# Wu products in 32-column tiles with two-block halo rows, against layers 1 and 2 on (row, channel) partitions

## The chip, the cores and the metric

The kernel runs on one core of one Trainium2 chip. The metric is the device time of one execution in microseconds (us); lower is better. The two kernels compute the same function; this document compares the kernel "before" with the kernel "after" that the diff below makes of it.

## The reference

The input x is 32 images of 8 channels and 256 x 256 pixels, float32. Four layers follow one another, each of the form x = x + f(groupnorm(x)) with four groups of two channels:

```python
# layer 0, on n = groupnorm(x)
grid = n
for _ in range(15):                       # the automaton, each channel by itself
    mapped = 3.9 * grid * (1 - grid)
    grid = 0.85 * (0.7 * mapped + 0.3 * conv3x3(mapped, K_local)) + 0.15 * n
cml = clip(grid)
nca = sigmoid(Wu @ relu(conv3x3(n, Wp) + bp) + bu)     # 8 -> 128 -> 8 channels
g = sigmoid(Wg2 @ relu(conv3x3([n, cml, nca], Wg1) + bg1) + bg2)
x = x + g * cml + (1 - g) * nca
x = x + conv3x3(quantize(groupnorm(x)), quantize(w1)) / scale + b1   # layer 1, scale over all of x
x = x + conv3x3(groupnorm(x), w2) + b2                              # layer 2
x = x + conv5x5(groupnorm(x), w3), every channel by itself          # layer 3
```

## The kernel before, in words

There are two stages. Layer 1 needs the largest absolute value over all images, so layer 0 of every image is finished first (stage 1, the first `with` block) and layers 1 to 3 follow (stage 2, the second block).

**Stage 1** has two streams of work, written as two generators. `lattice(b)` runs the automaton of image b. It loads the image into `xb` (L231), takes the statistics (L237 and `group_stats`, whose two small products are L94 and L101), writes the normalised image to DRAM (`xn_d`, `nr_d`), turns it to a layout of patches by transposes (L259) and does 15 steps. In a step each of the 8 channels gets two products, one with `patch_sb` (L281) and one with `ring_sb` (L282), and VectorE finishes the cell update (L289, L291). The rims of the patches travel by DMA from `state` to `rings` (`spread`, L221, on SyncE's queue). At the end the state is turned back (L302), copied into `xb` (L305) and written to DRAM (`cr_d`, L311).

`gated(b)` does the rest of layer 0. The image is cut into 16 blocks of 16 rows; `hidden(r2)` takes two blocks at a time. For each of the 16 row offsets it makes one product with Wp (L360: 72 rows of the moving tile `im`, out `ph` of 128 hidden channels x 512 pixels), ScalarE's Relu into `hh` (L365), and one product with Wu (L344). Wu has only 8 outputs, so before places them by a shifted window of a wide weight tile: all 16 offsets accumulate into one full 128-partition tile `pn`, each filling its 8 rows and adding zeros to the others. `gate(r2)` makes nine products with Wg1 (L393), two with the rows of the neighbouring blocks (L398 reads `ha`, L399 reads `hb`), one with Wg2 (L404), and the mixture on POOL and VectorE (L411 to L418). `beside_two` fills `hb` by DMA from `nh` (L321).

The two streams are woven: each `yield` of `lattice` carries a load, and the gated stream is advanced to 1.2 images behind. A scheduler then reorders the instructions of each engine by their expected times, so the order that runs isn't exactly the order written.

**Stage 2** keeps an image as (row, channel) on the partitions: partition 8 r + c holds channel c of row r of every block, the free axis holds the 16 blocks. A 3x3 convolution then takes three products with all 128 rows, one for each column shift (L499), and a fourth with a tile of 48 neighbouring rows that a DMA has gathered (`beside`, L128; product L503). So `conv3` is four products for each of eight chunks of 512 pixels, in bf16 for layer 1 and in float32 for layer 2. Layer 3 takes the image by whole rows (y, two halves of 128 rows): five products with `w3_sb` (L578) and a sixth with the few rows across the seam (`xr2`, L569 and L582). The output of layer 2 goes through DRAM (`x3_d`, L547) to get to that layout (`y`, L554). The loop runs layer 3 of image b-3, layer 2 of image b-1 and layer 1 of image b:

```python
for b in range(B + 3):
    if b >= 3:
        layer3(b - 3, *threes.pop(b - 3))
    if 1 <= b <= B:
        threes[b - 1] = layer2(b - 1, *twos.pop(b - 1))
    if b < B:
        twos[b] = layer1(b)
```

Of the kernel before, what the change touches and what calls it, by code (L numbers as in the profile page):

```python
# [9 lines left out]
F32 = mybir.dt.float32  # L10
BF16 = mybir.dt.bfloat16
# [49 lines left out]
def kernel(  # L61
    ctx, tc, x, patch, ring, wp, bp, wu, bu, wg1, wga, wgb, bg1, wg2, bg2, w1, b1, w2, b2, w3,
    w3h, eye, gavg, gavr, gsel, out,
# [12 lines left out]

    gavg_sb = const(keep, gavg, [P, P], "gavg_sb")
    gavr_sb = const(keep, gavr, [P, P], "gavr_sb")
# [8 lines left out]
    x3_d = [dram.tile([P, NPX], F32, name=f"x3_d{b}") for b in range(2)]  # L87
# [35 lines left out]
    def beside(queue, t, src, q):  # L123


        row, long = HB * WP, (HB - 1) * WP - 2
        for i, (p, to, at) in enumerate(((P - C, 1, 0), (0, 0, 1))):
            queue.dma_start(  # L128
                t[q + 24 * i : q + 24 * i + 24, :, :].rearrange("p k w -> p (k w)")[
                    :, to * WP : to * WP + long  # L130
                ],
                window(src, p * row + at * WP, [[row, C], [1, 3], [1, long]]),
            )
# [19 lines left out]
    with ExitStack() as es:  # L153
# [13 lines left out]
        wu_sb = const(wt, wu, [P, 2 * P - C], "wu_sb")  # L167
# [6 lines left out]
        bg2_sb = const(wt, bg2, [P, 1], "bg2_sb")  # L174

# [13 lines left out]
        nh = wt.tile([P, HB, WP], F32, name="nh")  # L189
        ha = wt.tile([96, HB, WP], F32, name="ha")  # L190
        hb = wt.tile([72, HB, WP], F32, name="hb")
        state = wt.tile([P, C, SN], F32, name="state")
        rings = [wt.tile([RING, 4, SN], F32, name=f"rings{i}") for i in range(2)]
        for t in (xb, nh, ha, hb, state, *rings):
            nc.gpsimd.memset(t, 0.0)
# [3 lines left out]
        xn_d = [dram.tile([C, HP, WP], F32, name=f"xn_d{i}") for i in range(3)]  # L199
        xr_d = [dram.tile([P, HB, W], F32, name=f"xr_d{i}") for i in range(3)]  # L200
        nr_d = [dram.tile([P, HB, WP], F32, name=f"nr_d{i}") for i in range(3)]
        cr_d = [dram.tile([P, HB, WP], F32, name=f"cr_d{i}") for i in range(3)]
# [24 lines left out]
        def lattice(b):  # L227
# [5 lines left out]
                on_rows(xr_d[b % 3], W), x[b].rearrange("c (k r) w -> (c k) r w", k=HB)  # L233
            )
            bn = small.tile([P, RB, 6], F32, name="bn0")
            for r in range(RB):
# [3 lines left out]
            yield 3  # L240
# [10 lines left out]
                window(xn_d[b % 3], WP, [[HP * WP, C], [RB * WP, HB], [1, RB * WP]]),  # L251
                xb.rearrange("p r w -> p (r w)"),
            )
            nc.gpsimd.dma_start(on_rows(nr_d[b % 3], WP), xb)
            yield 3
            for t4 in range(TX // 4):
                ps = psum.tile([P, 512], F32, name="ps")
                for j in range(4):
                    nc.tensor.transpose(  # L259
                        ps[:, bass.ts(j, P)], flat[:, bass.ts(4 * t4 + j, P)], eye_sb  # L260
                    )
                nc.scalar.copy(flat[:, bass.ts(t4, 512)], ps)
                if t4 % 4 == 3:
                    yield 0.5
# [9 lines left out]
            yield 1  # L274
            for step in range(STEPS):
                for half in range(2):
# [21 lines left out]
                    yield 1  # L298
            for t4 in range(TX // 4):
# [9 lines left out]
                if t4 % 4 == 3:  # L309
                    yield 0.5  # L310
            nc.gpsimd.dma_start(on_rows(cr_d[b % 3], WP), xb)  # L311

        LATTICE = 6 + 0.5 * TX // 16 + 1 + 2 * STEPS + 0.5 * TX // 16

        def beside_two(r2):

            row = HB * WP
            for i, (p, k0, to) in enumerate(((P - C, 2 * r2, 2 * r2 + 1), (0, 2 * r2, 2 * r2 - 1))):
                skip, last = max(0, -to), max(0, to + 2 - HB)
                long = (2 - skip - last) * WP - 2  # L320
                nc.sync.dma_start(  # L321
                    hb[24 * i : 24 * i + 24, :, :].rearrange("p k w -> p (k w)")[
                        :, (to + skip) * WP : (to + skip) * WP + long
                    ],
                    window(nh, p * row + (k0 + skip) * WP, [[row, C], [1, 3], [1, long]]),
                )

        def gated(b):
# [3 lines left out]
            xn, xr, nr, cr = xn_d[b % 3], xr_d[b % 3], nr_d[b % 3], cr_d[b % 3]  # L332
            beside(nc.gpsimd, ha, nr, 0)
            beside(nc.gpsimd, ha, cr, 48)
# [4 lines left out]
            def hidden(r2):  # L339
                pn = ps_n.tile([P, 512], F32, name="psn")  # L340
                late = None

                def second(hh, r):
                    nc.tensor.matmul(  # L344
                        pn, wu_sb[:, C * (RB - 1 - r) : C * (RB - 1 - r) + P], hh,
                        start=r == 0, stop=r == RB - 1,
                    )

                for half in range(2):
# [8 lines left out]
                    for j in range(8):  # L358
                        ph = psum.tile([P, 512], F32, name="ph", tag="ps")
                        nc.tensor.matmul(  # L360
                            ph.rearrange("p (k w) -> p k w", w=W), wp_sb,
                            im[:, :, j * WP : j * WP + W], start=True, stop=True,
                        )
                        hh = hp.tile([P, 512], F32, name="hh")
                        nc.scalar.activation(hh, ph, AF.Relu, bias=bp_sb)  # L365
                        if late is not None:
                            second(*late)
                        late = (hh, 8 * half + j)
                        yield
                second(*late)  # L370
                nc.scalar.activation(  # L371
                    nh[:, 2 * r2 : 2 * r2 + 2, 1 : 1 + W],
                    pn.rearrange("p (k w) -> p k w", w=W), AF.Sigmoid, bias=bu_sb,
                )
                beside_two(r2)
# [3 lines left out]
            def gate(r2):  # L379
                k0 = 2 * r2  # L380
                if r2 % 2 == 0:
# [9 lines left out]
                for s, src in enumerate((xq, cq, nh[:, k0 : k0 + 2, :])):  # L391
# [7 lines left out]
                nc.tensor.matmul(o, wgb_sb, hb[:, k0 : k0 + 2, 0:W], start=False, stop=True)  # L399
                g1 = hp.tile([P, 512], F32, name="g1", tag="hh")  # L400
# [4 lines left out]
                gt = hp.tile([P, 2, W], F32, name="gt", tag="hh")  # L405
                nc.scalar.activation(gt.rearrange("p r w -> p (r w)"), pq, AF.Sigmoid, bias=bg2_sb)  # L406
                ci = cq[:, :, 1 : 1 + W]
                ni = nh[:, k0 : k0 + 2, 1 : 1 + W]
# [18 lines left out]
            st = stat1[:, b, :]  # L427
# [6 lines left out]
            nc.vector.tensor_reduce(peak1[:, b : b + 1], ext2, AX.X, ALU.max, apply_absolute_value=True)  # L434
        GATED = NCH * (RB + 5)

        done = 0
        rest = (None for b in range(B) for _ in gated(b))  # L440
        for b in range(B):
            at = 0
            for load in lattice(b):
                at += load
                due = ((b - 1.2) * LATTICE + at) * GATED / LATTICE
                while done < due:
                    next(rest)
                    done += 1
        for _ in rest:
            pass  # L450


    with ExitStack() as es:
        wt = es.enter_context(tc.tile_pool(name="wt1", bufs=1))
        two = es.enter_context(tc.tile_pool(name="two", bufs=2))
        psum = es.enter_context(tc.tile_pool(name="ps_b", bufs=3, space=PSUM))
        ps_v = es.enter_context(tc.tile_pool(name="ps_v", bufs=5, space=PSUM))

        w1_sb = const(wt, w1, [P, 4, P], "w1_sb")
        b1_sb = const(wt, b1, [P, 1], "b1_sb")  # L460
        w2_sb = const(wt, w2, [P, 4, P], "w2_sb")
        b2_sb = const(wt, b2, [P, 1], "b2_sb")
        w3_sb = const(wt, w3, [P, 5, P], "w3_sb")
        w3h_sb = const(wt, w3h, [72, 2, P], "w3h_sb")
# [16 lines left out]
        w1_bf = wt.tile([P, 4, P], BF16, name="w1_bf")  # L481
        quantize(w1_bf.rearrange("p a b -> p (a b)"), w1f, sc[:, 1:2])


        qh = wt.tile([P, HB, WP], BF16, name="qh")
        qb = wt.tile([72, HB, WP], BF16, name="qb")
        xh = wt.tile([P, HB, WP], F32, name="xh")
        xb2 = wt.tile([72, HB, WP], F32, name="xb2")

        xr = wt.tile([P, 2, C, W + 4], F32, name="xr")  # L490
        xr2 = wt.tile([72, C, W + 4], F32, name="xr2")
        for t in (qh, qb, xh, xb2, xr, xr2):
            nc.gpsimd.memset(t, 0.0)

        def conv3(src, near, w, i):
            ps = ps_v.tile([P, 512], F32, name="psv")
            o = ps.rearrange("p (k w) -> p k w", w=W)
            for dx in range(3):
                nc.tensor.matmul(  # L499
                    o, w[:, dx, :], src[:, 2 * i : 2 * i + 2, dx : dx + W],  # L500
                    start=dx == 0, stop=False,
                )
            nc.tensor.matmul(  # L503
                o, w[0:72, 3, :], near[:, 2 * i : 2 * i + 2, 0:W], start=False, stop=True
            )
            return ps

        def layer1(b):
            x1 = two.tile([P, NPX], F32, name="x1")
            nc.gpsimd.dma_start(x1, x1_d[b])  # L510
            for k in range(4):
# [6 lines left out]
                    qh[:, 4 * k : 4 * k + 4, 1 : 1 + W],  # L518
                    t.rearrange("p (r w) -> p r w", w=W), sc[:, 0:1],
                )  # L520
            beside(nc.sync, qb, qh, 0)
            x2 = two.tile([P, NPX], F32, name="x2")
            bn = small.tile([P, NCH, 6], F32, name="bn")
            for i in range(NCH):
                ps = conv3(qh, qb, w1_bf, i)
                c = x2[:, bass.ts(i, 512)]
                nc.scalar.activation(c, ps, AF.Identity, bias=b1_sb, scale=sc[:, 3:4])
                nc.vector.tensor_tensor(c, c, x1[:, bass.ts(i, 512)], ALU.add)
                nc.vector.bn_stats(bn[:, i, :], c)
            st = small.tile([P, 2], F32, name="st2")  # L530
            group_stats(psum, bn, st, gavr_sb)
            return x2, st

        def layer2(b, x2, st):
            nc.vector.tensor_scalar(  # L535
                xh[:, :, 1 : 1 + W], x2.rearrange("p (k w) -> p k w", w=W),
                st[:, 0:1], st[:, 1:2], ALU.subtract, ALU.mult,
            )
            beside(nc.sync, xb2, xh, 0)
            bn = small.tile([P, NCH, 6], F32, name="bn")  # L540
            for i in range(NCH):
                ps = conv3(xh, xb2, w2_sb, i)
                c = x2[:, bass.ts(i, 512)]
                nc.vector.scalar_tensor_tensor(c, ps, b2_sb, c, ALU.add, ALU.add)
                nc.vector.bn_stats(bn[:, i, :], c)
            x3 = x3_d[b % 2]
            nc.gpsimd.dma_start(x3, x2)  # L547
# [185 lines left out]
```

## Time and profile before

| | us |
|---|---|
| median of three runs | 21494.88 |
| lowest and highest run | 21493.68 to 21496.85 |
| the profiled execution: its own time | 21493.68 |
| its span, first to last instruction | 21491.9 |
| stage 1, by the last product of layer 0 | 0 to 18940 |
| stage 2 | 18940 to 21492 |

The span is the profiler's; 1.8 us of the execution lie around it. PE is the engine of matrix products, PEld its weight load, DVE the vector engine, ACT the scalar engine, POOL and SP the two that mostly issue DMAs here. A float32 product shows as two MATMUL instructions, a bf16 product as one. "Busy" of PE counts from the start of a product to its modelled end and products overlap, so the time that a product costs is read from the distance between the starts of neighbours in the timeline, not from its mean duration.

### The profile page before, as it was taken

Reading aid. Unit: us, or ns where it says so; the run is one execution under the profiler, and the core shown is the slowest. Engines: PE = TensorE matmul, PEld = TensorE weight load, DVE = VectorE, ACT = ScalarE, POOL = GpSimd, SP = SyncE. Lnnn points to the kernel's source line nnn. Section 1 sums busy time; section 2 is a strip of 40 time slices with the busy share of each in tenths; the row PEclk is TensorE's granted clock in tenths of the full one; section 3 lists DMA queues with packets and bytes.
Section 4 is the critical chain, followed back from the end, with each engine's and each line's share of the span. In section 5 each row is a group of like instructions: output and inputs, shape, how many; then the busy total and the mean of one; then the engine's idle time right before and its main releaser. Section 6 shows DMA issues by size and latency. Waiting matters only on the chain.

```text
span 21491.9 us, 137690 instructions
## 1 busy us (share of the span) xinstructions
PE 19778.0 (92%) x46664; PEld 8662.7 (40%) x46664; DVE 8103.2 (38%) x13657; ACT 4075.8 (19%) x5790; POOL 1570.3 (7%) x1649
## 2 busy tenths in 40 slices
PE   6899999999999999999999999999999999989999
PEld 2343443434343444444343434344443434434444
DVE  4333333333333333333333333333333333245554
ACT  0111222212212111222222212121122222211110
POOL 0000000000000000000000000000000000011111
PEclk8999999999999999999999999999999999999999
DMA  5444444444444444444444444444444444345554
GB/s 112 104 104 105 103 109 106 107 108 108 105 109 106 108 103 106 105 105 108 105 110 107 107 106 108 107 106 102 105 106 108 107 107 105 84 106 126 126 126 109
DMA packets 525150, 2307.92 MB, mean 107 GB/s; under 512 B 111468, under 2 KB 179540, under 8 KB 356388
## 3 DMA queue, kind: packets, MB, share of 16 engines
q1 hardware_dynamic: 213668, 835.31, 21.3%
q10 hardware_dynamic: 172032, 810.61, 13.3%
q0 software_dynamic: 138752, 653.18, 11.5%
q8 instruction: 377, 6.18, 0.1%
q14 instruction: 321, 2.63, 0.0%
HBM read 1129.33 MB, written 471.38 MB: 74 GB/s over the span
## 4 chain that ended last, share of the span: by engine, by line
PE 79%; issue 8%; DMA 7%; DVE 3%; POOL 1%; ACT 1%; SPq 0%; ACTq 0%; POOLq 0%; DVEq 0%
PE ph L360 15%; PE psn L344 15%; PE psc L282 14%; PE psc L281 14%; PE pg L393 7%; PE psv L578 5%; PE psv L499 4%; DMA rings<-state 2%; DMA hb<-nh 2%; DMA xb<-in_x 1%; PE psv L503 1%; PE pq L404 1%; PE psv L582 1%; PE pg L399 1%; PE pg L398 1%
## 5 line engine op out<-in xcount | busy, mean ns | idle before, releaser
L289 DVE SCALAR_TENSOR_TENSOR state<-psc,dr 128x512 f32<-128x512 f32 x3840 | 2620.8, 689 | 7462.1 <-PE psc L282 5203.8
L365 ACT ACTIVATE hh<-ph,bp_sb 128x512 f32<-128x512 f32 x4096 | 2812.6, 687 | 8527.0 <-PE ph L360 7196.7
L360 PE MATMUL ph<-im,wp_sb 72*128 72x512 f32 x8192 | 4301.8, 622 | 26.6 <-DMA im<-xn_d 14.1
L282 PE MATMUL psc<-rings,ring_sb 80*128 80x512 f32 x7680 | 4006.9, 607 | 325.5 <-issue 271.6
L344 PE MATMUL psn<-hh,wu_sb 128*128 128x512 f32 x8192 | 4255.1, 612 | 21.8 <-ACT hh L365 21.7
L281 PE MATMUL psc<-state,patch_sb 128*128 128x512 f32 x7680 | 3932.0, 597 | 117.5 <-DVE state L289 115.5
L360 PEld LDWEIGHTS ph<-im,wp_sb 72*128 72x128 f32 x8192 | 1614.7, 199 | 2063.1 <-issue 1449.1
L344 PEld LDWEIGHTS psn<-hh,wu_sb 128*128 128x128 f32 x8192 | 1565.4, 194 | 2182.1 <-issue 1841.7
L291 DVE SCALAR_TENSOR_TENSOR state<-state 128x512 f32<-128x512 f32 x3584 | 2387.4, 695 | 30.5
L282 PEld LDWEIGHTS psc<-rings,ring_sb 80*128 80x128 f32 x7680 | 1478.6, 194 | 2215.4 <-issue 2194.8
L281 PEld LDWEIGHTS psc<-state,patch_sb 128*128 128x128 f32 x7680 | 1448.5, 190 | 2047.9 <-issue 1696.9
L413 DVE TENSOR_TENSOR gt<-gt,nh 128x512 f32<-128x512 f32 x256 | 177.9, 695 | 3176.7 <-POOL gt L412 3176.7
L412 POOL TENSOR_TENSOR gt<-gt,df 128x512 f32<-128x512 f32 x256 | 328.9, 1285 | 12404.6 <-ACT gt L406 11178.1
L578 PE MATMUL psv<-xr,w_sb 128*128 128x512 f32 x2560 | 1159.9, 595 | 0.5 <-DVE xr L563 0.5
L401 ACT ACTIVATE g<-pg,bg_sb 128x512 f32<-128x512 f32 x256 | 176.3, 689 | 3642.6 <-PE pg L399 3185.5
L94 PE MATMUL ps<-mv,gavg_sb 128*128 128x1 f32 x64 | 17.8, 348 | 785.1 <-DVE mv L92 785.1
L393 PE MATMUL pg<-xq,wg_sb 128*128 128x512 f32 x1536 | 713.4, 596 | 0.0
L499 PE MATMUL psv<-xh,w_sb 128*128 128x512 f32 x1536 | 704.1, 595 | 8.1 <-DVE xh L535 4.1
L578 PEld LDWEIGHTS psv<-xr,w_sb 128*128 128x128 f32 x2560 | 475.5, 189 | 565.5 <-issue 561.1
L393 PE MATMUL pg<-nh,wg_sb 128*128 128x512 f32 x1536 | 701.2, 592 | 0.0
L393 PE MATMUL pg<-cq,wg_sb 128*128 128x512 f32 x1536 | 701.0, 592 | 0.0
L411 POOL TENSOR_TENSOR df<-cq,nh 128x512 f32<-128x512 f32 x256 | 436.6, 1706 | 2127.7 <-ACT nh L371 2021.2
(132 smaller groups left out, 9430.8 us busy)
## 6 DMA issues: line engine op xcount, KB each, us to landing
im<-xn_d ACTq DMA_DIRECT2D x3072, 193.3 KB
rings<-state SPq DMA_DIRECT2D x1920, 213.8 KB
rings<-state SPq DMA_DIRECT2D x1920, 142.5 KB
xn_d<-xb POOLq DMA_DIRECT2D x32, 2064.0 KB, 23.6
nr_d<-xb POOLq DMA_DIRECT2D x32, 2064.0 KB, 29.4
xq<-nr_d ACTq DMA_DIRECT2D x128, 516.0 KB
cr_d<-xb POOLq DMA_DIRECT2D x32, 2064.0 KB, 11.2
cq<-cr_d ACTq DMA_DIRECT2D x128, 516.0 KB
```

The lines of the kernel that those rows point to most:

```text
L281: nc.tensor.matmul(o, patch_sb[:, c, :], v, start=True, stop=False)
L282: nc.tensor.matmul(o, ring_sb[:, c, :], rings[half][:, c % 4, 0 : TX * SY].rearrange("p (x y) -> p x y", y=SY)[:, :, 0:TY], start=False, s ...
L289: nc.vector.scalar_tensor_tensor(v, o, FLOOR, dr[:, c], ALU.max, ALU.add)
L291: nc.vector.scalar_tensor_tensor(v, v, 1.0, v, ALU.subtract, ALU.mult)
L344: nc.tensor.matmul(pn, wu_sb[:, C * (RB - 1 - r) : C * (RB - 1 - r) + P], hh, start=r == 0, stop=r == RB - 1,)
L360: nc.tensor.matmul(ph.rearrange("p (k w) -> p k w", w=W), wp_sb, im[:, :, j * WP : j * WP + W], start=True, stop=True,)
L365: nc.scalar.activation(hh, ph, AF.Relu, bias=bp_sb)
L393: nc.tensor.matmul(o, wg1_sb[:, s, dx, :], src[:, :, dx : dx + W], start=s == dx == 0, stop=False,)
L411: nc.gpsimd.tensor_tensor(df, ci, ni, ALU.subtract)
L412: nc.gpsimd.tensor_tensor(gt, gt, df, ALU.mult)
L499: nc.tensor.matmul(o, w[:, dx, :], src[:, 2 * i : 2 * i + 2, dx : dx + W], start=dx == 0, stop=False,)
L578: nc.tensor.matmul(o, w3_sb[:, dx, :], xr[:, k, 2 * g : 2 * g + 2, dx : dx + W], start=dx == 0, stop=False,)
```

## The change

The diff has five parts.

1. **Wu in column tiles** (`hidden`, `second`). The weight tile becomes four windows of 32 columns. The products of four row offsets go out together, two to partitions 32 q of `pn` and two to partitions 32 (q + 1), alternating between the two tiles. `hh` gets six buffers, and `g1`/`gt` a tag of their own with three.
2. **Halo rows for two blocks** (`beside_two`, `hbs`). `nh` gets an empty block at each end, and `hb` becomes two small tiles, each for the two blocks of one `gate`, filled at the start of `gate`.
3. **The weave** of stage 1: `gated(b - 1)` runs wholly inside `lattice(b)`, every `yield` weighing the same; the DRAM tiles go from three to two.
4. **Layers 1 and 2 by (channel, block)** on the partitions: partition 16 c + k. A 3x3 convolution is nine products, one for each tap, over 18 rows of which the first and last are fetched by `halo` (two products with a shift matrix and a ScalarE copy). The statistics of layer 0 are carried to that layout by a product with `tob`.
5. **Layer 3** takes ten products for each chunk (five with its own half, five with the other), in place of six; the loop runs layer 3 of image b-2; the loads and stores of stage 2 go to SyncE's queue, and `y` comes in two DMAs in place of sixteen.

```diff
-                def second(hh, r):
-                    nc.tensor.matmul(
-                        pn, wu_sb[:, C * (RB - 1 - r) : C * (RB - 1 - r) + P], hh,
-                        start=r == 0, stop=r == RB - 1,
-                    )
+                def second():
+                    for hh, r in late:
+                        q, i = divmod(r, 4)
+                        nc.tensor.matmul(
+                            pn[32 * q : 32 * q + 32, :], wu_sb[:, i, :], hh,
+                            start=i == 0, stop=i == 3,
+                        )
+                    late.clear()
...
-                    for j in range(8):
+                    for rows in ((0, 4, 1, 5), (2, 6, 3, 7)):
+                        four = []
+                        for i, j in enumerate(rows):
...
+                            hh = hp.tile([P, 512], F32, name="hh", bufs=6)
+                            nc.scalar.activation(hh, ph, AF.Relu, bias=bp_sb)
+                            four.append((hh, 8 * half + j))
+                            if i == 1:
+                                second()
+                            yield
+                        late += four
...
+        hbs = [wt.tile([72, 2, WP], F32, name=f"hb{i}") for i in range(2)]
+        def beside_two(hb, k0):
+            row, long = (HB + 2) * WP, 2 * WP - 2
+            for i, (p, at) in enumerate(((P - C, k0), (0, k0 + 2))):
                 nc.sync.dma_start(
+                    hb[24 * i : 24 * i + 24, :, :].rearrange("p k w -> p (k w)")[:, 0:long],
+                    window(nh, p * row + at * WP, [[row, C], [1, 3], [1, long]]),
                 )
...
-        rest = (None for b in range(B) for _ in gated(b))
-        for b in range(B):
-            at = 0
-            for load in lattice(b):
-                at += load
-                due = ((b - 1.2) * LATTICE + at) * GATED / LATTICE
-                while done < due:
+        for b in range(B + 1):
+            rest = gated(b - 1) if b > 0 else iter(())
+            done = 0
+            if b < B:
+                for i, _ in enumerate(lattice(b)):
+                    while done * LATTICE < GATED * (i + 1) and next(rest, rest) is None:
+                        done += 1
+            for _ in rest:
+                pass
...
+    def halo(psum, t, sh):
+        ps = psum.tile([P, 512], F32, name="ps")
+        nc.tensor.matmul(ps[:, 0:W], sh[:, 0, :], t[:, RB, 1 : 1 + W], start=True, stop=True)
+        nc.tensor.matmul(ps[:, W : 2 * W], sh[:, 1, :], t[:, 1, 1 : 1 + W], start=True, stop=True)
+        nc.scalar.copy(t[:, 0 : RB + 2 : RB + 1, 1 : 1 + W], ps.rearrange("p (r w) -> p r w", w=W))
...
-            for dx in range(3):
+            for tap in range(9):
+                dy, dx = divmod(tap, 3)
                 nc.tensor.matmul(
-                    o, w[:, dx, :], src[:, 2 * i : 2 * i + 2, dx : dx + W],
-                    start=dx == 0, stop=False,
-                )
-            nc.tensor.matmul(
-                o, w[0:72, 3, :], near[:, 2 * i : 2 * i + 2, 0:W], start=False, stop=True
-            )
+                    o, w[:, tap, :], src[:, 2 * r + dy : 2 * r + dy + 2, dx : dx + W],
+                    start=tap == 0, stop=tap == 8,
+                )
...
-            beside(nc.sync, qb, qh, 0)
+            halo(psum, q, shift_bf)
...
-            beside(nc.sync, xb2, xh, 0)
+            halo(psum, xh, shift_sb)
...
-            for k in range(HB):
-                nc.gpsimd.dma_start(
-                    y[RB * (k % 8) : RB * (k % 8) + RB, k // 8, :, :],
-                    window(x3, k * W, [[C * NPX, RB], [NPX, C], [1, W]]),
+            for k in range(2):
+                nc.sync.dma_start(
+                    y[:, k, :, :], x3[:, k * P : (k + 1) * P, :].rearrange("c p w -> p c w")
                 )
...
-                    for dx in range(5):
+                    for i, (part, dx) in enumerate((p_, d_) for p_ in range(2) for d_ in range(5)):
                         nc.tensor.matmul(
-                            o, w3_sb[:, dx, :], xr[:, k, 2 * g : 2 * g + 2, dx : dx + W],
-                            start=dx == 0, stop=False,
+                            o, w3_sb[:, 0 if part == 0 else 1 + k, dx, :],
+                            xr[:, k if part == 0 else 1 - k, 2 * g : 2 * g + 2, dx : dx + W],
+                            start=i == 0, stop=i == 9,
                         )
-                    nc.tensor.matmul(
-                        o, w3h_sb[:, k, :], xr2[:, 2 * g : 2 * g + 2, 0:W],
-                        start=False, stop=True,
-                    )
...
-        for b in range(B + 3):
-            if b >= 3:
-                layer3(b - 3, *threes.pop(b - 3))
+        for b in range(B + 2):
+            if b >= 2:
+                layer3(b - 2, *three_in)
```

## The prediction

> **What bounds the kernel now.** I read the page's 40 slices and the chain of waits first: PE is at 9 tenths nearly throughout and holds 79% of the chain. Then busy time in the two stages, cut at the last product of layer 0 (columns: stretch, its length, then busy us and count of PE, PEld, DVE, ACT, POOL, then granted clock, DMA share, GB/s):
>
> ```profile
> 424.00:18940.00 18516.00, 17039.72 (x39643) 7459.79 (x39643) 6507.38 (x10578) 3747.87 (x5330) 1157.51 (x1047) 0.94 0.45 105
> 18940.00:21492.00 2552.00, 2480.17 (x6472) 1101.62 (x6472) 1403.83 (x2767) 318.20 (x449) 378.50 (x580) 0.98 0.51 122
> ```
>
> PE is busy 92% of stage 1 and 97% of stage 2; no other engine passes 56%. A product's true cost I take from PE's timeline in stage 2, where nothing stands between the products (start, length, line, count):
>
> ```profile
> 20007.65 2.74 PE L499 MATMUL psv<-xh,w_sb 128*128 128x512 f32 x6
> 20010.23 1.02 PE L503 MATMUL psv<-xb,w_sb 72*128 72x512 f32 x2
> 20011.09 0.81 PE L499 MATMUL psv<-qh,w_bf 128*128 128x512 bf16 x3
> 20011.74 0.38 PE L503 MATMUL psv<-qb,w_bf 72*128 72x512 bf16 x1
> ```
>
> Six float32 passes take 20010.23 - 20007.65 = 2.58 us: 0.43 a pass, **0.86 us a float32 product** (two passes), with 72 rows as with 128. Three bf16 products take 0.65 us: **0.217 us each**. The mean durations in the groups (0.59 to 0.62) are longer, since neighbours overlap by 0.16 us; I don't multiply by them.
>
> What PE waits for (engine, line, releaser, total us, times, longest) and how it looks at the start of an image:
>
> ```profile
> PE ps L94 <- DVE mv L92: 797.1, 34, 39.5
> PE psc L282 <- issue: 271.6, 30, 11.0
> PE pg L399 <- DMA hb<-nh: 221.7, 28, 13.5
> ...
> 9138.52 0.56 PE L94 MATMUL ps<-mv,gavg_sb 128*128 128x1 f32 x2 [23.74 <-DVE mv L92]
> 9140.00 0.56 PE L101 MATMUL ps<-t,gavg_sb 128*128 128x1 f32 x2 [0.93 <-DVE t L99]
> 9140.43 3.76 PE L360 MATMUL ph<-im,wp_sb 72*128 72x512 f32 x4
> ```
>
> At each image PE stands 24 us until the next image has been loaded into `xb` and its statistics are there; the four passes after it take 3.55 us until the next start, not 1.72: half speed. The start of L94's wait to the next one is about 585 us in steady state: (17923.5 - 939.2) / 29, from the starts of that product. In stage 2 the waits of this list come to under 25 us in all: it is pure product time.
>
> **What the Trainium skill says.** "TensorE: Matmul & The Clock Gate", Part 3 (packing small matmuls): products on different column tiles run side by side (three tiles of 32 columns and 512 pixels measured 2.38 times faster), and products start and end in program order. "TensorEngine Tiling (Array Packing)", Key Properties: a change of tiling mode drains the engine; it gives no price. No run shown so far uses column tiles, so the trace says nothing on either. Part 1 of the first page: after an idle window of about 3.4 us the clock halves; the trace agrees (0.89 us a pass after the 23.74 us wait, against 0.43).
>
> **The change, part by part.** There are 32 images.
>
> *Stage 2, products (on the path).* Layer 1: 8 chunks x 9 = 72 bf16 in place of 32: +40 x 0.217 = +8.7 us an image. Layer 2: 72 float32 in place of 32: +40 x 0.86 = +34.4. Layer 3: 80 in place of 48: +32 x 0.86 = +27.5. The two `halo` calls, four products of half width: 0.2 + 0.9 = +1.1. Sum +71.7 us an image, **+2294 us**. VectorE had 1404 of 2552 us to do and gets nothing more, so nothing takes the bound from PE.
>
> *Stage 2, new waits.* Built, the order of PE after layer 2's last product is now L94, L101, L118, then `halo` of layer 1, then its products; in before layer 1's products of the next image stand between these small ones. So PE now waits out the chain of statistics. From DVE's timeline at an image's start: aggregate to finished statistics 3.6 us (9138.4 to 9142.0). With the last eviction and its statistics ahead (0.75 + 0.69 + 0.42, L544, L545, L92), the selection, L118 and `halo` with its copy (1.5): about 7.5 us. After such a gap the clock halves; the case above lost 4 to 5 us. The second `halo` costs about 0.9 (0.6 for the copy, by L262) and the statistics inside layer 3 0.5. Together 13.4 us, **+429 us**. Between 7 (no slow clock, 224 us) and 20 (640 us).
>
> *Stage 2, DMAs.* Gathering `qb`, `xb2`, `xr2` goes (six DMAs an image on SP) and costs nothing, since the work of other layers hid it. x1, x3 and y move from POOL to SP: x1, out twice, x3, y twice, in order; y waits for x3 to land (6.6 us) and x1 stands behind. Layer 3 now comes one image sooner: y must be there when layer 1 ends, 7.5 + 4.5 + 15.6 = 27.6 us after layer 2. x3 leaves at 2 and lands at 9; y's 2 MB then have 18 us (`xb`, also 2 MB, landed in 9.7). I take 0, with 10 us an image as the upper end (y sharing with x1, which took 21.2 before).
>
> *Stage 1, Wu.* Before: 4096 products x 0.86 = 3523 us. In after's built order the groups of four are partly torn: runs of four 521 times, three 280, two 322, one 528; 1651 runs. If a pass can run beside the next one when they are on different tiles, but the two passes of one product can't, a run of four takes 5 slots for 8, three 4 for 6, two 3 for 4, one 2: 521 x 5 + 280 x 4 + 322 x 3 + 528 x 2 = 5747 slots x 0.43 = 2471. **-1052 us**. Bounds: 0 (no overlap) and -1052.
>
> *Stage 1, mode changes.* Every run enters and leaves the tiled mode: 3302 changes. The trace has none. From below 0. From above the overlap that is lost, 0.16, and a weight load no longer hidden, 0.19 (L344 PEld, 194 ns): 0.35. I take the middle, 0.18: **+594 us**, between 0 and +1156.
>
> *Stage 1, the weave and the halo.* The load of `xb` still stands behind `cr_d` (11.1 + 9.7 us, then 5.3 + 0.6 of statistics), so the 24 us stay. `hb`'s wait (222 us, 28 times) falls in a time when `xn_d` and `nr_d` (2 MB each) are being written; after's gates of the last blocks stand ahead of these, so most of it may go. But less gated work covers the start of the automaton: between the transposes and the first L282-like product there are 12 products in place of 15, so its wait of about 10 us grows by 3 to 4. Net -4 us an image by these, and back for small stalls of torn groups waiting for `hh`: I take 0, within +-10 us an image (+-320). The product with `tob`, the third copy of the statistics and the changed constants lie in the 24 us wait; if it were gone they would cost 1 us an image.
>
> Sum on the profiled execution: 21493.7 + 2294 + 429 - 1052 + 594 = **23759**, say 23760. The median shown is 1.2 us above that execution, which changes nothing.
>
> **The rivals.**
> - *The tiles don't run side by side for float32* (two passes each with its own weights, or the mode serialises them): the -1052 is lost, the mode changes stay: 24811. For it: no trace shows the overlap, and half the gain is between two passes whose weights differ. Against: the page's 2.38.
> - *y comes late*: +10 us an image of PE wait, 24080. For it: layer 3 is one image nearer, and x1 and y share the DMA engines. Against: 0.51 DMA share in stage 2, and the stage now lasts twice as long.
> - *The other side, faster*: a column-tiled pass costs in proportion to its 32 columns. Then Wu's 8192 passes fall from 0.43 to 0.11, -2640, and overlap takes more. It decides the sign once the passes' cost falls by (2294 + 429) / 8192 = 0.33 us each, to 0.10; with the overlap too, 5747 slots x 0.1075 = 618, -2905, and without a price for mode changes 21312. Against: passes with 72 rows cost as much as with 128, and a bf16 pass half of a float32 one; the moving pixels set the time.
> - *That the change doesn't do what it says* is excluded: the built program has the 32-column products and the nine and ten products.
>
> **How the numbers follow.** The sum as worked out, 0.62 (its own range 23250 to 24300 by the bounds of the waits and mode changes); no overlap 0.22; late y 0.12; faster 0.03, and 0.01 for landing within 0.2%, about 43 us, which is what a measurement of this kernel can tell from no change. Slower 0.96. The range 23150 to 24850 takes in the middle of the no-overlap case and of late y, and leaves out its dear mode changes.
>
> **What would show it.** Right: stage 2 from about 2550 to 5250 us, with PE still near 90% busy; a wait of 6 to 8 us an image at L94 to L118; starts of Wu's products (L351) 0.43 us apart or closer in pairs, five slots to a group of four; stage 1 at about 18480. Wrong: Wu's products 0.86 apart (no overlap); a stage 1 above 19000; a wait of layer 3 for y; a stage 2 under 4950, which its products alone nearly fill.

## The result, and the profile after

The kernel after takes **24053.2 us** (median of four runs, 24041.2 to 24109.0) beside 21495.4 for the kernel before: ratio 1.1195, interval 1.1176 to 1.1214. The forecast was 23760 in a range of 23150 to 24850. It came out 293 us above the forecast. The two stages of the profiled execution (24041.2 us, span 24039.4) show that this is not one small miss (columns as before, cut at the last product of layer 0):

```profile
424.00:18905.00 18481.00, 16585.01 (x39702) 6358.48 (x39702) 6403.27 (x10596) 3681.01 (x5267) 1099.62 (x1043) 0.92 0.45 106
18905.00:24039.00 5134.00, 4876.94 (x12559) 2153.23 (x12558) 1492.10 (x2788) 385.19 (x516) 17.27 (x6) 0.97 0.15 53
```

Stage 2 went from 2552 to 5134 us, +2582, where the sum had +2723. Stage 1 went from 18940 to 18905, where the sum had it at 18480. (The last Wg2 product starts at 18927.1 in before and at 18904.7 in after, so 13 us of that difference lie in where the cut was made.) PE is busy 455 us less in stage 1 than before, and the stage is no shorter: the granted clock fell from 0.94 to 0.92, and the waits grew.

The boundary from layer 2 to the next layer 1 in stage 2, from PE's timeline (start, length, line; in brackets the wait before it and its releaser):

```profile
21059.80 39.65 PE L509 MATMUL psv<-xh,w_sb 128*128 128x512 f32 x92
21101.43 0.38 PE L94 MATMUL ps<-mv,gavg_sb 128*128 128x1 f32 x2 [1.98 <-DVE mv L92]
21102.65 0.38 PE L101 MATMUL ps<-t,gavg_sb 128*128 128x1 f32 x2 [0.84 <-DVE t L99]
21104.76 0.59 PE L118 MATMUL ps<-sel,ones 128*128 128x8 f32 x2 [1.72 <-DVE sel L116]
...
21106.47 17.47 PE L509 MATMUL psv<-qh,w_bf 128*128 128x512 bf16 x72 [0.68 <-ACT qh L128]
21123.77 2.74 PE L583 MATMUL psv<-xr,w_sb 128*128 128x512 f32 x6
```

The last pass of layer 2 starts at 21059.80 + 39.65 - 0.59 = 21098.86 and ends 0.43 later; layer 1 starts at 21106.47. PE stands 7.2 us but for the small products. The 72 bf16 products then take 21123.77 - 21106.47 = 17.3 us, 1.7 more than 72 x 0.217.

A group of four products with Wu in stage 1:

```profile
9023.98 1.02 PE L279 MATMUL psc<-rings,ring_sb 80*128 80x512 f32 x2
9024.93 1.91 PE L351 MATMUL psn<-hh,wu_sb 128*32 128x512 f32 x8
9026.77 1.13 PE L370 MATMUL ph<-im,wp_sb 72*128 72x512 f32 x2
9027.74 1.88 PE L278 MATMUL psc<-state,patch_sb 128*128 128x512 f32 x4
```

Eight passes take 1.84 us, four slots of 0.43 and 0.12 more. So the two float32 products of a pair run side by side entirely (in the trace their passes start 6 to 7 ns apart). The passes before the group take 0.95 for 0.86, those after it 0.97: entering and leaving the tiled mode costs some 0.09 + 0.12 + 0.11 = 0.32 us a group. The group is typical: of the 521 whole groups in the trace the median takes 1.841 us.

What PE waits for now:

```profile
PE psc L278 <- DVE state L286: 581.6, 293, 8.9
PE ps L94 <- DVE mv L92: 550.7, 96, 37.4
PE ph L370 <- DMA im<-xn_d: 261.8, 25, 14.8
```

The first line is new at this size: the automaton's product waits for VectorE's update of `state`. In before this stood at:

```profile
PE psc L281 <- DVE state L289: 115.5, 127, 4.8
```

What VectorE waits for at that place is in its own list, first in before, then in after:

```profile
DVE state L289 <- DMA rings<-state: 2075.6, 343, 13.7
```

```profile
DVE state L286 <- DMA rings<-state: 3069.8, 491, 21.2
```

An update of `state` needs the `rings` through its own product only. But it waits for a *copy out of* `state`, as a writer that must not overtake a reader. In the built program the first update of a half (channels 0 to 3 or 4 to 7) waits on the semaphores of two of the four ring copies that `spread` has just issued for the *other* half: both halves lie in one tile. After's timeline shows it:

```profile
9072.81 2.75 SPq L218 DMA_DIRECT2D rings<-state  x4
...
9074.56 2.74 PE L279 MATMUL psc<-rings,ring_sb 80*128 80x512 f32 x6
...
9081.54 1.29 DVE L286 SCALAR_TENSOR_TENSOR state<-psc,dr 128x512 f32<-128x512 f32 x2 [8.80 <-DMA rings<-state]
...
9082.29 2.08 PE L278 MATMUL psc<-state,patch_sb 128*128 128x512 f32 x2 [4.99 <-DVE state L286]
...
9084.16 1.91 PE L279 MATMUL psc<-rings,ring_sb 80*128 80x512 f32 x2
```

The copies of one half go out at 9072.81; the other half's products are done by 9077.3, but its first update starts only at 9081.54, and PE has stood 5 us. (In the trace the last count of the second copy's semaphore comes at 9081.02, and VectorE's wait for it ends at 9081.05.) The next two passes take 1.87 us in place of 0.86: half clock. The two halves, meant to cover each other's copies, are strung one behind the other. The kernel before has this too; there it hardly reached PE.

### The profile page after: what moved, and what is told of

Same layout as the page of the kernel before. It is cut to its first block, busy times and chain, and to the rows that moved or that the text cites. A ratio compares the mean times of both kernels' runs of the same rounds, so it can differ in the third digit from the quotient of the medians.

```text
span 24039.4 us, 145434 instructions
## 1 busy us (share of the span) xinstructions
PE 21730.1 (90%) x52808; PEld 8619.8 (36%) x52808; DVE 8083.0 (34%) x13690; ACT 4075.7 (17%) x5794; POOL 1148.0 (5%) x1072
## 4 chain that ended last, share of the span: by engine, by line
PE 78%; DMA 11%; DVE 7%; issue 1%; ACT 1%; POOL 1%; SPq 1%; DVEq 0%; ACTq 0%; POOLq 0%
PE ph L370 14%; PE psc L278 13%; PE psc L279 12%; PE psv L509 10%; PE psn L351 9%; PE psv L583 9%; PE pg L405 8%; DMA rings<-state 7%; DMA xb<-in_x 2%; DMA im<-xn_d 1%; PE pq L416 1%; DVE state L286 1%; PE pg L411 1%; POOL gt L424 1%; DVE xc L426 1%
## 5 line engine op out<-in xcount | busy, mean ns | idle before, releaser
L286 DVE SCALAR_TENSOR_TENSOR state<-psc,dr 128x512 f32<-128x512 f32 x3840 | 2569.5, 687 | 7976.4 <-PE psc L279 4536.1
L278 PE MATMUL psc<-state,patch_sb 128*128 128x512 f32 x7680 | 3920.1, 624 | 584.1 <-DVE state L286 581.6
L279 PE MATMUL psc<-rings,ring_sb 80*128 80x512 f32 x7680 | 3958.2, 621 | 129.2 <-DMA rings<-state 128.0
L351 PE MATMUL psn<-hh,wu_sb 128*32 128x512 f32 x8192 | 2538.8, 628 | 0.0
L583 PE MATMUL psv<-xr,w_sb 128*128 128x512 f32 x5120 | 2221.9, 593 | 6.9 <-DVE xr L573 6.9
L509 PE MATMUL psv<-xh,w_sb 128*128 128x512 f32 x4608 | 1989.0, 593 | 23.7 <-ACT xh L128 23.7
L583 PEld LDWEIGHTS psv<-xr,w_sb 128*128 128x128 f32 x5120 | 961.0, 189 | 1202.0 <-issue 1197.5
L509 PEld LDWEIGHTS psv<-xh,w_sb 128*128 128x128 f32 x4608 | 868.7, 189 | 1130.7 <-issue 1093.8
L351 PEld LDWEIGHTS psn<-hh,wu_sb 128*32 128x32 f32 x8192 | 431.2, 111 | 1837.6 <-issue 1835.4
L405 PE MATMUL pg<-xq,wg_sb 128*128 128x512 f32 x1536 | 789.5, 623 | 0.0
L555 DVE SCALAR_TENSOR_TENSOR x<-psv,b_sb,x 128x512 f32<-128x512 f32 x256 | 192.2, 751 | 1678.4 <-PE psv L509 1678.4
```

What stands on the lines that cost most here:

```text
L278: nc.tensor.matmul(o, patch_sb[:, c, :], v, start=True, stop=False)
L279: nc.tensor.matmul(o, ring_sb[:, c, :], rings[half][:, c % 4, 0 : TX * SY].rearrange("p (x y) -> p x y", y=SY)[:, :, 0:TY], start=False, s ...
L286: nc.vector.scalar_tensor_tensor(v, o, FLOOR, dr[:, c], ALU.max, ALU.add)
L351: nc.tensor.matmul(pn[32 * q : 32 * q + 32, :], wu_sb[:, i, :], hh, start=i == 0, stop=i == 3,)
L405: nc.tensor.matmul(o, wg1_sb[:, s, dx, :], src[:, :, dx : dx + W], start=s == dx == 0, stop=False,)
L509: nc.tensor.matmul(o, w[:, tap, :], src[:, 2 * r + dy : 2 * r + dy + 2, dx : dx + W], start=tap == 0, stop=tap == 8,)
```

## The experiments

The first four runs set **weave** (the new order of the two streams makes the waits) against a first form of **chain** (the automaton's ring copies and the load of the next image set some 580 us an image, whatever TensorE has to do). From e5 on two theories were set against each other. **Chain:** the halves' ring copies, one after the other, bound stage 1 at about its present length, so what TensorE saves turns into waits. **Order:** the products stand in a fixed order on TensorE, and the groups of four are lumps that make it wait whatever the chain does.

All times are medians, of four runs or more but for e4 (two); ratios are to the kernel before on the same chip (21501 to 21506 us).

**e1, the column tiles alone**: before with parts 1 and 2 of the diff.

```diff
+        hbs = [wt.tile([72, 2, WP], F32, name=f"hb{i}") for i in range(2)]
...
+                        nc.tensor.matmul(
+                            pn[32 * q : 32 * q + 32, :], wu_sb[:, i, :], hh,
+                            start=i == 0, stop=i == 3,
+                        )
```

> Parts 1 and 2 alone on the kernel before (Wu in column tiles, halo rows for two blocks). In after's trace Wu's products and what follows a change of tiling mode cost 30 us an image less than in before (112 to 72 us for Wu's own starts, +9.5 for the passes after a change). Theory 'weave' (the new order of the two streams of stage 1 made the waits that ate this): about 21495 - 970 = 20500 to 20700. Rival 'chain' (the automaton's own chain of rims by DMA, and the load of the next image, set some 580 us an image whatever the PE has to do): 21350 to 21500.

Measured: 21900.6, ratio 1.0181 (1.0166 to 1.0196). Both expectations missed: the tiles, which take time from PE, cost 395 us. PE's list shows on what (before has 797.1, 115.5 and 51.2 us on these three):

```profile
PE ps L94 <- DVE mv L92: 859.5, 34, 37.7
PE psc L281 <- DVE state L289: 824.2, 348, 9.4
PE psc L282 <- DMA rings<-state: 270.4, 60, 20.5
```

**e2, the weave alone**: before with part 3's loop, the DRAM tiles left at three.

```diff
+            rest = gated(b - 1) if b > 0 else iter(())
...
+                for i, _ in enumerate(lattice(b)):
+                    while done * LATTICE < GATED * (i + 1) and next(rest, rest) is None:
```

> Part 3 alone on the kernel before (gated(b - 1) wholly inside lattice(b), every yield of the same weight). Theory 'weave': the waits and slow passes that after has more of, 29 us an image, come with it: about 22400. Rival 'chain': the period of an image stays near 585 us: 21450 to 21650.

Measured: 20866.1, 0.9704 (0.9688 to 0.9721). Both expectations missed: the weave is a gain of 640 us by itself, so it didn't make the waits, and an image isn't held at 585 us. The gain lies at the start of an image. Of the first 120 us from L94's first product on, 36 were more than PE's own work in before and 13 are in e2 (images 8 to 30). The wait before the first L282 ("issue", 271.6 us in before) has gone from the list, and that for `hb`, 221.7 us in before, has shrunk:

```profile
PE ph L360 <- DMA hb<-nh: 57.5, 20, 5.3
...
PE pg L399 <- DMA hb<-nh: 15.7, 12, 2.7
```

**e3, after with before's weave** (part 3 undone).

```diff
-        for b in range(B + 1):
-            rest = gated(b - 1) if b > 0 else iter(())
...
+                due = ((b - 1.2) * LATTICE + at) * GATED / LATTICE
```

> The kernel after with the weave of before (part 3 undone: gated 1.2 images behind, weighted yields, three DRAM tiles). Theory 'weave': stage 1 gets the 29 us an image back: about 24050 - 930 = 23120. Rival 'chain': 23950 to 24100.

Measured: 24584.3, 1.1431 (1.1414 to 1.1448), 531 above after. Both expectations missed here too; the weave is worth about as much in the kernel after.

**e4, after with six products in layer 3** and the seam tile of before.

```diff
-                    for i, (part, dx) in enumerate((p_, d_) for p_ in range(2) for d_ in range(5)):
+                    for dx in range(5):
...
+                        o, w3h_sb[:, k, :], xr2[:, 2 * g : 2 * g + 2, 0:W],
```

> The kernel after with layer 3's six products in place of ten (only that of part 5 undone). Both theories: stage 1 as in after; stage 2 loses 32 products x 0.86 us an image, 880 us in all, if PE alone bounds stage 2: about 23170. If the small transfers of the seam rows (81 KB, two an image) now stand in the way, 23250 to 23400.

Measured: 23204.3, 1.0790 (1.0768 to 1.0811), 849 below after. The term of the sum for these 32 products an image, 32 x 27.5 = 880, stands.

**e5, after with the state in two tiles**, one for each half. No arithmetic changes; the wait for the other half's copies goes. The built order changes with it, since the scheduler has one dependency less: in images 10 to 14, 280 of PE's 1258 passes an image stand in another place.

```diff
-        state = wt.tile([P, C, SN], F32, name="state")
+        states = [wt.tile([P, 4, SN], F32, name=f"state{i}") for i in range(2)]
...
+            return states[c // 4][:, c % 4, AT : AT + TX * SY]
...
+            state = states[half]
-                at = p * row + 4 * half * SN + AT + far
+                at = p * row + AT + far
```

> The kernel after, with the automaton's state held in two tiles, one for each half of the rows, in place of one. No arithmetic changes; what goes is a wait: with one tile the first update of a half waits for ring copies that were issued for the other half. Theory chain (the two halves' ring copies, one after the other, set how long an image takes in stage 1, so time saved on TensorE turns into waits): the waits of the automaton's products for the state's updates, some 580 us in the kernel after, go for the most part, stage 1 falls by 600 to 900 us and the kernel takes 23150 to 23450. Theory order (the products stand in a fixed order on TensorE and the groups of four are lumps in it, so it waits whatever the chain does): 23950 to 24100, as the kernel after.

Measured: 23092.7, 1.0735 (1.0717 to 1.0753), **960 us below after**. The wait of the automaton's product for an update in a step is no longer in PE's list (581.6 before the split), and VectorE's wait for ring copies at the step's update went from 3069.8 us to 161.9; VectorE now waits for the product instead (4536.1 us in after):

```profile
DVE state L287 <- PE psc L280: 7850.5, 2181, 27.6
...
DVE state L287 <- DMA rings<-state: 161.9, 25, 11.2
```

This is chain, and a little more than it expected. By the table below an image is 31.2 us shorter, 20 of them waits and 10 half clock, and the wait that went had 581.6 of the 960 us. What the new order adds by itself wasn't run apart.

**e6, the split with the new weave and Wu as before** (e2 with e5's edit).

```diff
+        states = [wt.tile([P, 4, SN], F32, name=f"state{i}") for i in range(2)]
```

> The kernel before with the weave of the change (e2) and the state in two tiles. In e2 the waits of the automaton's products for the state came to only 85 us, so both theories expect little: 20700 to 20870. It is the base to which the next kernel is compared.

Measured: 20861.4, 0.9702 (0.9688 to 0.9717), the same as e2. With full-width Wu and the new weave the false dependency costs nothing.

**e7, weave, column tiles and split together**, stage 2 as before.

```diff
+        states = [wt.tile([P, 4, SN], F32, name=f"state{i}") for i in range(2)]
...
+                            pn[32 * q : 32 * q + 32, :], wu_sb[:, i, :], hh,
```

> The kernel before with the weave of the change, the column tiles for Wu with their halo held for two blocks, and the state in two tiles; layers 1 to 3 of stage 2 as before. Theory chain: with the chain of ring copies halved, the 900 us or so that the column tiles save on TensorE are seen at last: 19700 to 20000, some 900 below e6. Theory order: the groups cost what they cost in the kernel after beside e2, and it takes 21200 to 21500.

Measured: 20462.4, **0.9519** (0.9503 to 0.9534), the fastest of all kernels here. It is 399 below e6: the sign that chain expects, and less than half the size.

**e8, the groups without the narrow products**: before with e1's halo, groups and order, but each product over all 128 columns.

```diff
                         nc.tensor.matmul(
-                            pn[32 * q : 32 * q + 32, :], wu_sb[:, i, :], hh,
-                            start=i == 0, stop=i == 3,
+                            pn, wu_sb[:, C * (RB - 1 - r) : C * (RB - 1 - r) + P], hh,
+                            start=r == 0, stop=r == RB - 1,
                         )
```

> The kernel before with the halo held for two blocks and Wu's products in the groups of four and the order of the change, but each as one product of 128 columns, as before, so that none lies beside another and no change of mode is paid. It tells what the grouping costs by itself. Theory order: the lumps alone make TensorE wait some 1000 us more, 22500 to 23000. Theory chain: the groups are of little weight, and the chain has slack only for what TensorE saves: 21500 to 21700.

Measured: 21535.0, 1.0015 (1.0008 to 1.0022). The lumps cost 34 us, not a thousand: **order falls.** The products that the program groups in the same way cost 366 us more when they are made faster (e1). As built the two orders aren't the same: of the 1024 groups 853 stay whole in e8 and 576 in e1, so e8 has the larger lumps. And PE's wait for `state`, 824.2 us in e1, is what it was in before:

```profile
PE psc L281 <- DVE state L289: 105.0, 95, 6.0
```

**e9 and e10, the split with before's weave**, without and with the column tiles. Edits: e5's on before, and e5's on e1.

```diff
+        states = [wt.tile([P, 4, SN], F32, name=f"state{i}") for i in range(2)]
```

> The kernel before with the state in two tiles and nothing else. In the kernel before TensorE waits only 115 us for the state's updates, but the weave alone (e2) gave 640 us. If what the weave gave was slack for the chain of ring copies, the split gives much of the same: 20850 to 21100. If the weave gave evenness that the split can't give: 21400 to 21500.

Measured: 21548.1, 1.0023 (1.0015 to 1.0030), 47 us slower than before. The split gives nothing here, so the weave's 640 us aren't slack for the chain.

> The kernel e1 (before with the column tiles for Wu and their halo held for two blocks, the weave as before) with the state in two tiles. Theory chain: the 390 us that the column tiles cost in e1 turn into a gain of 300 to 500 us against the kernel with the split alone (e9). The rival, that the narrow products themselves cost it by their mode changes and a lower clock: it stays 300 us or more above e9.

Measured: 21174.3, 0.9847 (0.9830 to 0.9863): 374 below e9, 726 below e1. The column tiles' loss of 395 has turned into a gain by one edit that leaves PE's products as they are, though not their order (360 of 1256 passes of an image stand elsewhere), and the rival (the narrow products cost by themselves) falls. VectorE's wait for ring copies at the update is 525.2 us (2726.8 in e1), and PE's wait for `state` (L281 in e1, L282 here) has left the top of PE's list:

```profile
PE ps L94 <- DVE mv L92: 860.8, 34, 37.8
PE pg L403 <- DMA hb<-nh: 353.9, 91, 10.3
PE psc L283 <- DMA rings<-state: 334.8, 109, 20.6
```

**e11, e7 with Wu at full width** in the same groups.

```diff
-                            pn[32 * q : 32 * q + 32, :], wu_sb[:, i, :], hh,
+                            pn, wu_sb[:, C * (RB - 1 - r) : C * (RB - 1 - r) + P], hh,
```

> The kernel e7 with Wu's products at their full width of 128 columns, in the same groups and order. It parts what the groups and the halo cost from what the narrow products bring once the chain is loose. Both theories: 20850 to 20950, as e6; then the narrow products bring some 400 to 480 us net, 900 by TensorE's own time less what comes back as waits and slow passes. If it comes out below 20700, the grouping is a gain by itself and the narrow products bring less.

Measured: 20801.3, 0.9670 (0.9656 to 0.9685). That is 49 us below what was expected. So the narrow products bring 339 us of e7, groups and halo 60.

**e12, e7 with the next image's statistics taken early**, from x loaded a second time in four pieces.

```diff
+                if b + 1 < B and 2 <= step < 10:
+                    if step % 2 == 0:
+                        xs = fetch(b + 1, step // 2 - 1)
+                    else:
+                        measure(b + 1, step // 2 - 1, xs)
...
+            st = stx[b]
+            yield 3
```

> The kernel e7 with the statistics of the next image's x taken during the image before, from four pieces of x that are loaded a second time, and one more slot of the weave between the load of x and its use. What goes is the wait of TensorE for the mean and variance at the start of every image, 551 us in e7 (31 of some 17.5 us). If nothing else is late there: 19900 to 20050. If the transposes that follow wait for the load of x in its place, or the images' first blocks for the normalised x: 20300 to 20450.

Measured: 20686.3, 0.9622 (0.9608 to 0.9637), **224 slower than e7** and above both expectations. The wait for the mean fell from 551 to 239 us, but `im` is late in its place:

```profile
PE ph L387 <- DMA im<-xn_d: 359.5, 40, 13.6
PE ph L387 <- issue: 324.6, 31, 17.7
PE ps L94 <- DVE mv L92: 238.6, 33, 54.9
```

The DMA share (last but one column) just after the start of an image, beside a stretch of the image before:

```profile
8800.00:8850.00 50.00, 49.22 (x139) 19.69 (x138) 14.18 (x26) 9.44 (x14) 3.52 (x3) 1.00 0.38 118
8860.00:8880.00 20.00, 14.13 (x24) 5.35 (x24) 7.21 (x25) 5.61 (x8) 4.56 (x7) 0.54 0.95 265
8900.00:8920.00 20.00, 4.01 (x7) 1.65 (x7) 0.00 (x0) 2.33 (x3) 1.63 (x2) 0.57 0.54 182
```

From 8860 to 8880 `cr_d` and x, 2 MB each, and the rows for `ha` are on their way (0.95 of the DMA engines' time). `xn_d` and `nr_d`, 2 MB each, leave at 8886 and take 25.5 and 35.0 us, and from 8900 to 8920 PE is busy 4 us of 20. What PE no longer waits for the mean comes back as waits at the product that reads `im`. Whether the transfers hold `im`, or ScalarE's queue does, wasn't parted. The second load of x adds to the traffic, too.

**All of stage 1 in one table.** For images 8 to 30 I took the distances between the starts of neighbouring passes on PE in each trace, us an image. Of each distance 0.43 at most is own work (a distance up to 0.45 counts as own work whole). What a distance has above that is a small stall or mode change if the distance is 0.45 to 0.80, half clock if 0.80 to 1.02, a wait if longer.

| kernel | image | own work | small, modes | half clock | waits |
|---|---|---|---|---|---|
| before | 585.4 | 518.9 | 4.3 | 14.8 | 47.4 |
| e8: groups, full width | 587.0 | 518.6 | 2.5 | 18.3 | 47.6 |
| e9: split | 586.2 | 518.8 | 4.6 | 13.9 | 48.9 |
| e1: column tiles | 597.7 | 474.0 | 17.5 | 34.1 | 72.1 |
| e10: column tiles, split | 576.1 | 473.0 | 14.7 | 33.2 | 55.2 |
| e2: weave | 565.9 | 518.4 | 5.0 | 6.8 | 35.7 |
| e11: weave, split, groups | 563.0 | 518.3 | 1.6 | 10.2 | 32.9 |
| after | 583.8 | 476.8 | 16.6 | 28.4 | 62.0 |
| e5: after, split | 552.6 | 476.3 | 15.9 | 18.4 | 42.0 |
| e7: weave, column tiles, split | 549.8 | 475.5 | 15.9 | 16.2 | 42.2 |

The own work falls by 42 to 46 us an image wherever Wu is in column tiles, as it should. Small stalls and mode changes take back 10 to 15. The rest is decided by waits and half clock: with the false dependency they take all that is left and more (e1 beside e8, after beside e2), without it a half (e7 beside e11) to three quarters (e10 beside e9). And a wait costs more than its length: between 5000 and 17500 us, 76 to 97% of the half-clock passes of these kernels start within 12 us after a distance of over 1.5 us. The Trainium skill, "TensorE: Matmul & The Clock Gate", Part 1, has the clock halve after an idle window of about 3.4 us. The traces agree for most of these passes, and in part not: only 53 to 84% of them start within 12 us after an idle time of over 3.4 us, and the three gaps in stage 2, of 2.0, 0.8 and 1.7 us, each below that window, were followed by slower passes too (17.3 us for 15.6).

## Why the prediction was right or wrong

The range and the sign held. The terms of the sum can be judged one by one.

- **Stage 2, products, +2294: right.** Layer 3's part was forecast at 880 and measured at 849 (e4). Nothing else became the bound.
- **Stage 2, new waits, +429: too large.** The chain of statistics was forecast at 7.5 us and took 7.2. The half clock after it was the mis-sized part: 1.7 us (1.8 in the mean of 31 images) where I took 4 to 5 from the case of a 24 us wait. The gaps here are 2.0, 0.8 and 1.7 us. That is some 2.8 x 32 = 90 us of the 141 that stage 2 came out below its forecast.
- **Wu, overlap, -1052: the mechanism right, the size too small.** I let the two passes of one product lie apart, five slots for a group of four. They take four: (521 x 4 + 280 x 4 + 322 x 2 + 528 x 2) x 0.43 = 4904 x 0.43 = 2109 us in place of 3523, so -1414, outside the bound of -1052 that I gave. The own work in the table, 42 us an image, says the same. The Trainium skill, "TensorE: Matmul & The Clock Gate", Part 3, has products on different tiles side by side; here that holds for float32 pairs in full.
- **Mode changes, +594: about right.** 0.32 us a run, 1651 runs, 528 us; 10 to 15 us an image in the table, 320 to 480 us in all. The bound from above, 1156, is excluded. This is the price for which "TensorEngine Tiling (Array Packing)", Key Properties, gives none.
- **The weave and the halo, 0 within +-320: wrong.** The weave alone is worth -640 (e2), and -531 in the kernel after (e3). I had both waits at the start of an image before me, and took the one before the first L282 (271.6 us) to grow by 3 to 4 us an image, where e2 loses it, and left out the half clock behind both: 14.8 us an image in before, 6.8 in e2.
- **The step that failed: that time taken from PE in stage 1 is time taken from the stage.** I argued that PE is busy 92% of stage 1 and added up PE's savings. But the automaton's chain of update, ring copies, and the other half's update was close behind PE's own work, as e1, e5 and e10 show together. The sign of it stood in the list of all engines' waits that I had asked for, in a line that I passed over: VectorE's 2075.6 us for ring copies, at an update that reads none. In place of -458 for Wu, the column tiles cost 395 us with before's weave (21900.6 against 21505.9), and 605 in stage 1 with the new one (18300 in e2 to 18905 in after, which also has the `tob` product and two DRAM tiles in place of three).

These last two errors had opposite signs. In stage 1 the weave brought some 640 us that the sum didn't have, and the column tiles missed their -458 by 605 + 458 = 1063: together 423 above the forecast of 18480, and stage 2 gave 141 back. So the hit is partly luck: two terms were wrong by more than the error of the sum. The range that I gave for the sum alone, 23250 to 24300, was narrower than its own bounds: waits of 224 to 640 and mode changes of 0 to 1156 make it 22960 to 24530.

Of the rivals, "no overlap" is excluded by the starts of the passes, the faster side by eight passes in four slots of 0.43 (a pass isn't cheaper for its 32 columns), and "y comes late", 24080, landed nearest by its number and is false: layer 3's products waited 6.9 us in all.

What stays open: why the column tiles with the serial chain make an image *longer* (597.7) and not only no shorter. The automaton's own products lie on the chain and run at half clock after waits like the one at 9082, so waits may lengthen what causes them. The traces show both halves of that loop, but no run cut it. Nor was the split run with the built order held as it was.

## What to carry to other kernels

Before adding up savings on the busiest engine, look in the waits of the engines beside it for an instruction that waits for something whose result it doesn't read. Two halves in one tile, one written while the other is still being copied out, are such a dependency. Here it cost nothing (e6, e9) until the busy engine got faster. When a saving disappears, split the shared tile and time that alone: the edit adds and removes no work. But compare the built order too, since a scheduler may use the new freedom. Count a wait on TensorE with the passes at half clock behind it.

## What the runs showed of the hardware that I had not expected

Column-tiled float32 pairs overlap completely, with both passes: 8 passes in 1.84 us. Their weight loads, 32 columns each, take 111 ns in the mean beside 189 to 208 for 128 columns in the same kernel. A product alone in its run gains nothing: its two passes take 0.98 us until the next start, one after the other.

And half-clock passes follow short idle times too. I took, from the ten traces of the table between 5000 and 17500 us, each idle time of PE with neither a half-clock pass nor a distance of over 1.5 us in the 12 us before it, and looked for a half-clock pass within 4 us after it. After 1.1 to 1.5 us idle one followed 21 times of 239, after 1.5 to 2.0 us 43 of 137, after 2.0 to 2.5 us 47 of 75, and after 2.5 to 3.4 us 56 of 59. Such gaps add up: after has 28.4 us an image of half clock with 251 distances of over 1.5 us in that stretch, e2 6.8 with 75.
